# A decoder layer on one core: the first norm's result turned in 32 by 32 blocks on VectorE and through DRAM, and the contraction in quarters

## The chip, the core and the metric

One core of one Trainium2 chip runs the whole kernel. The metric is the device time of one execution in microseconds (us). The engines are TensorE (PE), VectorE (DVE), ScalarE (ACT), GpSimd (POOL) and SyncE (SP), which issues most of the DMAs. Each takes the instructions of its own queue in order.

## The reference

A post-norm decoder layer in float32 over 16 sequences of 512 tokens with 256 features (16 heads of 16; 1024 hidden units). Cut to what matters:

```python
q = query @ wq + query @ Aq @ Bq * 4.0
k = query @ wk
v = query @ wv + query @ Av @ Bv * 4.0
scores = rope(q) @ rope(k).T / sqrt(16)            # per head, causal
a = softmax(scores) @ v @ wo
x1 = layernorm(query + a)                          # the first norm
h = butterfly(x1 @ W_exp + b_exp, up_weights)      # 10 stages over 1024
h = gelu(h + up_bias)
h = butterfly(h, down_weights)
y = h @ W_con + b_con + down_bias
out = layernorm(x1 + y)                            # the second norm
```

## The kernel before

The linear butterflies are folded into the two dense matrices once, at the start (`fold_tasks`), so that each sequence, called a batch, needs x1 times a 256x1024 matrix (`wup`), a gelu, and a 1024x256 matrix (`wdn`).

**Slots.** The order of everything is written out by hand. The loop at the end of `decoder_layer` runs over slots s. A batch begins every 20 slots (`per`), and slot s holds, in this order: the score matmuls of two quads of heads, `largest` (for the row maxima, into the PSUM pair tile `pa` or `pb`) and, 15 slots behind, `weights` (for the exponentials); then `weigh`, which multiplies exponentials into `po`; then the list `others[s]`, filled by `add`; then the list `holes[s]`. Batch b starts at s = 20 b, its attention is finished at s+40, and its feed-forward part runs at s+40 to s+68, beside the attention of the next two batches. The engines keep this order: no scheduler moves anything.

**Scores.** `pa` and `pb` are one buffer each (pools `ps_a`, `ps_b`, bufs=1). Of a `largest` block the VectorE custom reduction L426 reads the scores and leaves a maximum in `mx` (the tile named `junk` is its discarded output); ACT's exponential L488 reads the `weights` blocks, and POOL's select L492 masks them. Slots go round in fives: two with one 512-wide block, two with 384 and 128, one with two of 256, which use both banks for both kinds.

**First norm.** `project_out` (PE) makes attention times `wo` for a tile of 128 tokens, `add_attention` adds it to the tile `z` and takes the statistics (VectorE), `spread` adds epsilon on VectorE and takes the power -0.5 on POOL, `offset` makes -mean/deviation on VectorE, and `centre` applies both on ACT, 4 tiles. The result is x1 with tokens on the partitions. `wup` needs it with features on the partitions: that is `turn_x1`. It makes 4 transposes of 128x128 on PE for each of two halves of the features, one VectorE copy each into `x1T`, and then a POOL add of the output bias to `z`.

**Feed-forward.** `hidden` makes one of 8 chunks of 128 hidden units on PE (8 matmuls of 512 columns), copied to `h` by VectorE (chunks 0 and 4) or ACT; `gelus` runs over all chunks at s+50; `contract` makes a tile of 128 tokens in two halves of 4 chunks, 16 matmuls of 256 columns each, in `py`, and after the second half VectorE adds `py` to `z` and takes the statistics of the second norm. `project_v` makes a tile of the values for a later batch (PE, with a copy by ACT).

**SyncE's queue.** Around s+41 to s+46 it carries, for the next batch, `rows` and `qz<-rows` (row maxima by way of DRAM, L446 and L452), then `sums<-x` and `x<-x` (L546, L550, after ACT has copied `po`), `few<-sums` (L558), and, after a VectorE reciprocal (L564), `recips`, `wide` and `spread` (L566 to L574). PSUM's pool `ps_w` for all other products has 3 buffers.

Of the kernel before, what the change touches and what calls it, by code (L numbers as in the profile page):

```python
# [11 lines left out]
F32 = mybir.dt.float32  # L12
BF16 = mybir.dt.bfloat16
AF = mybir.ActivationFunctionType
ALU = mybir.AluOpType
PSUM = bass.MemoryType.PSUM

P = 128
NH = 16
DH = 16  # L20
HG = 32
NG = P // HG
# [11 lines left out]
def decoder_layer(  # L34
# [18 lines left out]
    nc = tc.nc  # L53
    B, T, D = x.shape
    NT = T // P
    NC = D // P
    DHID = wcon.shape[0]
    NHC = DHID // P
# [5 lines left out]
    ring2 = ctx.enter_context(tc.tile_pool(name="ring2", bufs=2))  # L64
# [3 lines left out]
    dram = ctx.enter_context(tc.tile_pool(name="dram", bufs=4, space=bass.MemoryType.DRAM))  # L68
# [5 lines left out]
    def bank(name, shape):  # L74
        return ps_w.tile(shape, F32, tag="w", name=name)

    def columns(out, w, moving, start, stop):

        for g in range(NG):
            part = slice(HG * g, HG * (g + 1))  # L80
            nc.tensor.matmul(out[part, :], w[:, part], moving, start=start, stop=stop)  # L81
# [10 lines left out]
    xTs, zs = {}, {}  # L92
# [23 lines left out]
    wdn = const.tile([P, NHC, D], F32, name="wdn")  # L116
    bias2 = const.tile([P, 2, D], F32, name="bias2")
# [337 lines left out]
    state = {}  # L455
# [151 lines left out]
    def stats_of(which, b, t):  # L607
        if t == 0:
            state["stats", which, b] = small.tile(
                [P, NT, 2], F32, tag=f"stats{which}", name=f"stats{which}_{b}"  # L610
            )
        bn = small.tile([P, nc.vector.BN_STATS_DIM], F32, tag="bn", name=f"bn{which}_{b}_{t}")
        nc.vector.bn_stats(bn, zs[b][:, t, :])
        nc.vector.bn_aggr(state["stats", which, b][:, t, :], bn)
# [13 lines left out]
    def offset(which, b, t0=0, t1=NT):  # L628
        stats, norm = state["stats", which, b], state["norm", which, b]
        ts = slice(t0, t1)  # L630
        nc.vector.scalar_tensor_tensor(  # L631
            norm[:, 2, ts], stats[:, ts, 0], -1.0, norm[:, 1, ts], ALU.mult, ALU.mult
        )
# [10 lines left out]
            )  # L644


    def turn_x1(b, c):
        if c == 0:
            state["x1T", b] = ring2.tile([P, NC, T], F32, tag="x1T", name=f"x1T_{b}", bufs=1)
        pt = bank(f"pt1_{b}_{c}", [P, NT, P])  # L650
        for t in range(NT):
            nc.tensor.transpose(pt[:, t, :], zs[b][:, t, c * P : (c + 1) * P], ident)  # L652
        nc.vector.tensor_copy(
            state["x1T", b][:, c, :], pt.rearrange("p t q -> p (t q)")
        )
        if c == NC - 1:
            nc.gpsimd.tensor_tensor(
                zs[b],
                zs[b],
                bias2[:, 0:1, :].to_broadcast([P, NT, D]),  # L660
                ALU.add,
            )

    def hidden(b, hc, fused=False):
        if hc == 0:
            state["h", b] = hpool.tile([P, NHC, T], F32, tag="h", name=f"h_{b}")
        ph = bank(f"ph_{b}_{hc}", [P, T])
        for c in range(NC):
            columns(
                ph,  # L670
                wup[:, c, hc * P : (hc + 1) * P],
                state["x1T", b][:, c, :],
                c == 0,
                c == NC - 1,
            )
        h = state["h", b][:, hc, :]
        if fused:
            nc.scalar.activation(h, ph, AF.Gelu, bias=hbias[:, hc : hc + 1])  # L678
        elif hc % 4 == 0:
            nc.vector.tensor_copy(h, ph)  # L680
        else:
            nc.scalar.copy(h, ph)  # L682
# [5 lines left out]
                h[:, hc, :], h[:, hc, :], AF.Gelu, bias=hbias[:, hc : hc + 1]  # L688
            )

    def contract(b, t, half):
        if half == 0:
            state["py"] = bank(f"py_{b}_{t}", [P, D])
        py = state["py"]
        for hc in range(half * NHC // 2, (half + 1) * NHC // 2):
            columns(
                py,
                state["h", b][:, hc, t * P : (t + 1) * P],
                wdn[:, hc, :],
                hc == 0,  # L700
                hc == NHC - 1,
            )
        if half == 1:
            nc.vector.tensor_add(zs[b][:, t, :], py, zs[b][:, t, :])  # L704
            stats_of(2, b, t)

    def store(b):
        nc.sync.dma_start(out[b].rearrange("(t p) d -> p t d", p=P), zs[b])
# [14 lines left out]
    end = B * per + behind  # L723
    last = end + 8
    head = 2
    others = {s: [] for s in range(-head, last)}
    holes = {}
    chains = [(c, side) for c in range(NC) for side in range(2)]

    def add(s, f, *args):  # L730
        others[s].append(lambda: f(*args))

    def start_projection(b, side, c):
        state["pr", b, side, c] = project(b, side, c)
# [13 lines left out]
    for b in range(B):  # L748
        s = b * per
        if b > 0:  # L750

            at = {1: (-16, -11, -13, -9), B - 1: (-3, 2, 10, 10)}.get(b, (-3, -1, 2, 12))
            for t in range(NT):
                add(s + at[t], project_v, b, t)
        if b + 1 < B:

            add(s - head * (b == 0), load_xT, b + 1)
            at = {0: (2, 5, 7, 10), 1: (3, 6, 8, 11)}.get(b, (10, 10, 10, 10))
            for i, (c, side) in enumerate(chains):
                holes.setdefault(s + at[i], []).append(  # L760
                    lambda b=b, side=side, c=c: start_projection(b + 1, side, c)
                )
                turning = s + max(at[0] + 1 + 3 * i, at[i] + 1)
                for step in range(3):
                    add(turning + step, turn, b + 1, side, c, step)
                for step in range(1 + side):
                    add(turning + (6 if i == 3 else 4) + step, part, b + 1, side, c, step)
        add(s + 9, load_x, b)
        add(s + 11, place_largest, b, 0)
        add(s + 21, place_largest, b, 1)  # L770
        for c in range(NC if b + 1 < B else 1):
            if c + 1 < NC:
                add(s + 25 + (b + 1 == B), gather, b, c)
            add(s + (26, 36)[c] + (b + 1 == B), invert, b, c)
            for t in range(NT):
                add(s + ((29, 29, 30, 30), (39, 39, 40, 40))[c][t], scale, b, c, t)
        if b + 1 < B:
            for t in range(NT):
                add(s + (40, 40, 41, 41)[t], project_out, b, t)
                add(s + (40, 40, 41, 42)[t], add_attention, b, t)  # L780
            add(s + 42, spread, 1, b)
            others[s + 43].insert(0, lambda b=b: offset(1, b))
            add(s + 44, centre, 1, b)
            for c in range(NC):
                add(s + 45 + (b + 2 == B), turn_x1, b, c)
        if b + 2 < B:

            late = 2 * (b + 3 == B)
            for hc in range(NHC - late):
                add(s + 46 + hc // 2, hidden, b, hc)  # L790
            holes.setdefault(s + 50, []).insert(0, lambda b=b, late=late: gelus(b, NHC - late))
            for hc in range(NHC - late, NHC):
                holes[s + 50].append(lambda b=b, hc=hc: hidden(b, hc, True))
            for t in range(NT):
                for half in range(2):
                    at = (11, 13, 14, 15, 16, 18, 23, 24)[2 * t + half]
                    if b + 3 == B and t == NT - 1:
                        at = (23, 25)[half]
                    add(s + 40 + at, contract, b, t, half)
            add(s + 65, spread, 2, b)  # L800
            add(s + 67, offset, 2, b)
            add(s + 68, centre, 2, b)
            add(s + 68, store, b)
# [3 lines left out]
    y, z = B - 2, B - 1  # L807
# [4 lines left out]
    for hc, at in ((3, 10), (4, 10), (5, 10), (6, 11), (7, 11)):  # L812
        add(edge + at, hidden, y, hc, True)

    add(end - 3, contract, y, 0, 0)
    add(end - 1, contract, y, 0, 1)
    add(end + 2, contract, y, 1, 0)
    add(end + 2, contract, y, 1, 1)
    for t in range(NT):
        add(end + 2, normalize, z, NC - 1, t)  # L820
    add(end + 2, contract, y, 2, 0)
    for t in range(NT + 1):
        if t < NT:
            add(end + 3, project_out, z, t)
# [2 lines left out]
        if t > 0:  # L827
            add(end + 3, offset, 1, z, t - 1, t)
            add(end + 3, centre, 1, z, t - 1, t)
    add(end + 3, contract, y, 2, 1)  # L830
    add(end + 3, contract, y, 3, 0)
    for c in range(NC):
        add(end + 5, turn_x1, z, c)
    add(end + 5, contract, y, 3, 1)
    for hc in range(NHC):
        add(end + 5, hidden, z, hc, True)
    add(end + 5, spread, 2, y)
# [2 lines left out]
    add(end + 6, store, y)  # L840
    for t in range(NT):
        for half in range(2):
            add(end + 7, contract, z, t, half)
        add(end + 7, finish_tile, z, t)


    first, second = fold_tasks()
# [180 lines left out]
```

## Time and profile before

| | |
|---|---|
| runs | median 1318.08 us of 3 (1312.0 to 1320.54) |
| profiled execution | 1318.97 us, span 1317.0 us, mean granted clock 0.989 |
| busy: PE, DVE, ACT, POOL | 1280.6, 780.5, 702.9, 565.1 us |
| a steady batch | 76.60 us, PE busy 76.37 us |
| transposes L652 | 128, 273 ns each by the median; eight take PE from 552.64 to 553.66 us in batch 5 |
| copies L653 | 32, 678 ns each by the median |

Times in the lines below are us from the start of the span: start, duration, engine, line, operation, output and inputs, shapes, and a count where neighbours are merged; in brackets the idle time before and what ended it. "PEld" is the weight load, "SPq" a DMA issue on SyncE's queue. Matmuls overlap in the array, so starts tell more than durations.

### The profile page before, as it was taken

The page shows a single profiled execution, that of the slowest core. Times are in us where ns is not written, and L with a number is a line of the kernel's source. Part 1 is how long each engine was busy: PE and PEld are TensorE (multiplying, and loading weights), DVE is VectorE, ACT ScalarE, POOL GpSimd, SP SyncE. Part 2 cuts the span into 40 slices and gives each one's busy share as a digit, 9 for nine tenths or more (in the row PEclk, how much of TensorE's full clock was granted, in tenths as well). Part 3 has the DMA queues.
Part 4 walks back from the last instruction along what each step waited for, and adds up shares of the span by engine and source line. Part 5 has one row for each costly group of instructions (what it writes and reads, how often), then busy time and mean ns, then how long its engine had stood idle before and what let it go on. Part 6 is the DMA issues. An engine that isn't in the chain of part 4 may idle for free.

```text
span 1317.0 us, 38318 instructions
## 1 busy us (share of the span) xinstructions
PE 1280.6 (97%) x15896; PEld 575.2 (44%) x15896; DVE 780.5 (59%) x2760; ACT 702.9 (53%) x1047; POOL 565.1 (43%) x905
## 2 busy tenths in 40 slices
PE   8888999999999999999999999999999999999998
PEld 3343435444353544435354443535444353444443
DVE  5776746657465665747566574756657474665431
ACT  2574455555646555564655546465555646455643
POOL 4525325445362544536254453625445362532430
PEclk9889999999999999999999999999999999999999
DMA  5411111111212111121211112121211212111101
GB/s 169 132 32 59 40 49 46 56 56 41 82 41 65 47 56 56 41 83 41 69 42 57 56 41 83 41 67 45 56 56 40 83 41 70 41 40 32 43 20 34
DMA packets 64062, 74.07 MB, mean 56 GB/s; under 512 B 23120, under 2 KB 42576, under 8 KB 63888
## 3 DMA queue, kind: packets, MB, share of 16 engines
q1 hardware_dynamic: 60000, 66.07, 16.0%
q10 hardware_dynamic: 3888, 5.55, 1.4%
q8 instruction: 125, 2.05, 0.7%
q14 instruction: 49, 0.40, 0.1%
HBM read 40.17 MB, written 18.06 MB: 44 GB/s over the span
## 4 chain that ended last, share of the span: by engine, by line
PE 92%; DVE 3%; ACT 2%; DMA 1%; issue 1%; POOL 0%; SPq 0%; POOLq 0%; DVEq 0%; ACTq 0%
PE pb L474 21%; PE py L81 17%; PE ph L81 16%; PE po L516 12%; PE pqk L81 8%; PE pa L417 4%; PE pwo L81 4%; PE pvv L81 4%; DVE junk L426 1%; PE pd L81 1%; PE pt L652 1%; PE pa L474 1%; PE pb L417 1%; ACT pT L488 1%; ACT h L687 0%
## 5 line engine op out<-in xcount | busy, mean ns | idle before, releaser
L426 DVE CUSTOM_DVE_ANT_0 junk<-pa,causal 128x384 bf16<-128x384 f32 (+2 forms) x878 | 438.6, 500 | 339.0 <-PE pa L417 271.6
L488 ACT ACTIVATE pT<-pb 128x1024 f32<-128x1024 f32 (+1 forms) x314 | 294.2, 937 | 354.8 <-PE pa L417 183.8
L492 POOL TENSOR_SCALAR_AFFINE_SELECT pT<-pT 128x256 f32<-128x256 f32 x512 | 202.3, 407 | 651.4 <-ACT pT L488 650.4
L474 PE MATMUL pb<-qz,kz 17*128 17x512 f32 (+2 forms) x1756 | 330.9, 475 | 17.6 <-ACT pT L488 11.7
L417 PE MATMUL pa<-kz,qz 32*128 32x384 f32 (+3 forms) x1756 | 330.6, 476 | 3.4 <-DVE mx L426 3.4
L81 PE MATMUL py<-wdn,h 128*32 128x256 f32 x4096 | 244.3, 381 | 0.0
L81 PE MATMUL ph<-x1T,yb 128*32 128x512 f32 x2048 | 231.6, 594 | 0.2 <-ACT h L678 0.2
L474 PEld LDWEIGHTS pb<-qz,kz 17*128 17x128 f32 (+1 forms) x1756 | 142.4, 184 | 196.4 <-issue 92.3
L516 PE MATMUL po<-pT,vaug 128*32 128x512 f32 (+3 forms) x2048 | 180.9, 447 | 1.8 <-POOL pT L492 1.8
L81 PEld LDWEIGHTS py<-wdn,h 128*32 128x32 f32 x4096 | 125.3, 110 | 99.2 <-issue 12.7
L417 PEld LDWEIGHTS pa<-kz,qz 32*128 32x128 f32 (+1 forms) x1756 | 143.2, 185 | 14.6 <-DVE mx L426 11.6
L81 PEld LDWEIGHTS ph<-x1T,yb 128*32 128x32 f32 x2048 | 63.2, 110 | 139.8 <-issue 107.6
L81 PE MATMUL pqk<-xT,wqk 128*32 128x512 f32 x1024 | 117.6, 608 | 0.0
L682 ACT COPY h<-ph 128x512 f32<-128x512 f32 x84 | 49.2, 585 | 117.3 <-PE ph L81 117.2
L516 PEld LDWEIGHTS po<-pT,vaug 128*32 128x32 f32 x2048 | 47.9, 109 | 105.3 <-issue 59.1
L426 DVE DVE_READ_ACCUMULATOR2_ANT mx<- 128x1 f32 x1024 | 84.6, 83 | 0.0
L638 ACT ACTIVATE z<-z,norm 128x256 f32<-128x256 f32 x128 | 66.7, 589 | 23.2 <-DVE norm L631 23.2
L365 POOL TENSOR_TENSOR swap<-swap,rope_sb 128x512 f32<-128x512 f32 x62 | 78.8, 1270 | 0.0
L426 DVE CUSTOM_DVE_ANT_0 junk<-pb,causal 128x256 bf16<-128x256 f32 (+3 forms) x146 | 63.6, 436 | 16.4 <-PE pb L417 2.5
L687 ACT ACTIVATE h<-h,hbias 128x512 f32<-128x512 f32 x113 | 70.8, 709 | 0.2
L704 DVE TENSOR_TENSOR z<-py,z 128x256 f32<-128x256 f32 x64 | 27.2, 425 | 72.9 <-PE py L81 70.6
L81 PE MATMUL pvv<-wv_sb,xT 128*32 128x256 f32 x1024 | 66.5, 379 | 0.0
(91 smaller groups left out, 1192.1 us busy)
## 6 DMA issues: line engine op xcount, KB each, us to landing
xT<-in_xT SPq DMA_DIRECT2D x16, 512.0 KB
swap<-qz SPq DMA_DIRECT2D x64, 128.0 KB
swap<-kz SPq DMA_DIRECT2D x64, 128.0 KB
z<-in_x SPq DMA_DIRECT2D x16, 512.0 KB
wide<-recips SPq DMA_DIRECT2D x31, 256.0 KB
spread<-wide SPq DMA_DIRECT2D x31, 256.0 KB
out_y<-z SPq DMA_DIRECT2D x15, 512.0 KB
x<-x SPq DMA_DIRECT2D x32, 128.0 KB
```

Of the source, the lines that this page charges most:

```text
L81: nc.tensor.matmul(out[part, :], w[:, part], moving, start=start, stop=stop)
L365: engine.tensor_tensor(swap, swap, rope_sb[:, 1, :], ALU.mult)
L417: lambda i=i, rows=rows, at=at, n=n, t=t, ps=ps: nc.tensor.matmul(ps[:, i, at : at + n], q[rows, par, t * P : n], k_[rows, par, 0:n], star ...
L426: lambda i=i, at=at, n=n, t=t, g=g, ps=ps: nc.vector.tensor_tensor_reduce(out=junk[:, 0:n], in0=ps[:, i, at : at + n], in1=causal[:, T - n ...
L474: lambda i=i, rows=rows, at=at, n=n, k=block, ps=ps: nc.tensor.matmul(ps[:, i, at : at + n], kt[rows, par, k * P : (k + 1) * P], qt[rows, ...
L488: nc.scalar.activation(pT[:, heads, 0:n], ps[:, :, at : at + n], AF.Exp)
L492: nc.gpsimd.affine_select(out=diag, in_=diag, pattern=[[0, 2], [1, P]], compare_op=ALU.is_ge, fill=0.0, base=0, channel_multiplier=-1,)
L516: nc.tensor.matmul(po[HG * g : HG * (g + 1), k * P : T], vaugs[b % 2][:, k, NG * c + g, first : first + HG], pT[:, g, at : at + n], start= ...
L638: nc.scalar.activation(zs[b][:, t, :], zs[b][:, t, :], AF.Identity, bias=norm[:, 2, t : t + 1], scale=norm[:, 1, t : t + 1],)
L682: nc.scalar.copy(h, ph)
L687: nc.scalar.activation(h[:, hc, :], h[:, hc, :], AF.Gelu, bias=hbias[:, hc : hc + 1])
L704: nc.vector.tensor_add(zs[b][:, t, :], py, zs[b][:, t, :])
```

## The change

`turn_x1` is replaced for all batches but the last by `turn_blocks` and `fetch_turned`. `turn_blocks` turns all of `z` on VectorE in one instruction, which transposes each 32 by 32 block in place of the grid; partition j of a group of 32 then holds the features j, 32+j, 64+j and so on for the group's 128 tokens, and four DMAs write them to a DRAM tile in pieces of 512 bytes, one DMA a group. `fetch_turned` reads the DRAM tile back into `x1T` in pieces of 2 KB, with features on the partitions. The tokens lie in another order in `x1T` and so in `h`; `contract` picks its columns by an access pattern.

The steps of the first norm stand in slots 40 and 41 (`add_attention`, two tiles each), 41 (`spread`), 42 (`offset`), 43 (`centre`) and 44 (`turn_blocks`), counted from s; the fetch stands among the holes of slot 45. Before, the last `add_attention` and `spread` stood in 42, `offset` at the head of 43, `centre` in 44 and `turn_x1` in 45 (46 for batch 14). The hidden chunks go from slots 46 to 49 (two each) to the holes of 47, 48 and 49 (2, 3, 3; for batch 13, which has six here, 2, 2, 2). The contraction goes in 16 quarters in place of 8 halves, and three `project_v` of a later batch move. In the built program SyncE's queue has, after `qz<-rows`: four writes `x1rows<-turned`, `sums<-x`, `x<-x`, `few<-sums`, then the fetch `x1T<-x1rows`, then `recips`. VectorE's queue has in slot 44: four reductions L426, the add of `py` of the batch before with its statistics, the turn; then slot 45's reductions. In slot 41 it has the reductions, two adds with statistics, `spread`'s add and the turn of the maxima (`mT`).

```diff
+    def turn_blocks(b):
+
+        state["x1T", b] = ring2.tile([P, NC, T], F32, tag="x1T", name=f"x1T_{b}", bufs=1)
+        turned = ring2.tile([P, D // HG, NT, HG], F32, tag="turned", name=f"turned_{b}", bufs=1)
+        nc.vector.transpose(turned, zs[b].rearrange("p t (k j) -> p k t j", j=HG))
+        rows = dram.tile([D, NG, P], F32, tag="x1rows", name=f"x1rows_{b}")
+        state["x1rows", b] = rows
+        for g in range(NG):
+            nc.sync.dma_start(
+                rows.rearrange("(k j) g q -> j k g q", j=HG)[:, :, g, :],
+                turned[HG * g : HG * (g + 1)].rearrange("j k t i -> j k (t i)"),
+            )
+        nc.gpsimd.tensor_tensor(
+            zs[b],
+            zs[b],
+            bias2[:, 0:1, :].to_broadcast([P, NT, D]),
+            ALU.add,
+        )
+
+    def fetch_turned(b):
+        rows = state.pop(("x1rows", b))
+        nc.sync.dma_start(state["x1T", b], rows.rearrange("(c p) g q -> p c (g q)", p=P))
...
-    def contract(b, t, half):
-        if half == 0:
+    def contract(b, t, first, past):
+        if first == 0:
...
+        h = state["h", b]
+        if b + 1 == B:
+            of = h.rearrange("p c (t g i) -> p c t g i", g=NG, i=HG)
+        else:
+            of = h.rearrange("p c (g t i) -> p c t g i", g=NG, i=HG)
+        for hc in range(first, past):
+            for g in range(NG):
+                nc.tensor.matmul(
+                    py[HG * g : HG * (g + 1), :],
+                    of[:, hc, t, g, :],
+                    wdn[:, hc, :],
+                    start=(hc == 0),
+                    stop=(hc == NHC - 1),
+                )
+        if past == NHC:
...
-            at = {1: (-16, -11, -13, -9), B - 1: (-3, 2, 10, 10)}.get(b, (-3, -1, 2, 12))
+            at = {1: (-16, -11, -13, -9), B - 1: (-3, 2, 10, 10)}.get(b, (-1, 5, 6, 6))
...
-                add(s + (40, 40, 41, 42)[t], add_attention, b, t)
-            add(s + 42, spread, 1, b)
-            others[s + 43].insert(0, lambda b=b: offset(1, b))
-            add(s + 44, centre, 1, b)
-            for c in range(NC):
-                add(s + 45 + (b + 2 == B), turn_x1, b, c)
+                add(s + (40, 40, 41, 41)[t], add_attention, b, t)
+            add(s + 41, spread, 1, b)
+            add(s + 42, offset, 1, b)
+            add(s + 43, centre, 1, b)
+            add(s + 44, turn_blocks, b)
+            holes.setdefault(s + 45, []).append(lambda b=b: fetch_turned(b))
...
-                add(s + 46 + hc // 2, hidden, b, hc)
+                at = s + ((47, 47, 48, 48, 49, 49) if late else (47, 47, 48, 48, 48, 49, 49, 49))[hc]
+                holes.setdefault(at, []).append(lambda b=b, hc=hc: hidden(b, hc))
...
-            for t in range(NT):
-                for half in range(2):
-                    at = (11, 13, 14, 15, 16, 18, 23, 24)[2 * t + half]
-                    if b + 3 == B and t == NT - 1:
-                        at = (23, 25)[half]
-                    add(s + 40 + at, contract, b, t, half)
+            for n, at in enumerate((11, 11, 12, 13, 13, 14, 15, 16, 16, 17, 18, 18, 22, 23, 23, 24)):
+                add(s + 40 + at, contract, b, n // 4, n % 4 * 2, n % 4 * 2 + 2)
```

The last two batches keep the halves, by a helper `halves` that calls `contract` for four chunks.

More of the change, by code (lines that the diff above doesn't have):

```diff
@@ L689, in gelus, with halves @@
             )
-    def contract(b, t, half):
-        if half == 0:
+    def contract(b, t, first, past):
+        if first == 0:
             state["py"] = bank(f"py_{b}_{t}", [P, D])
         py = state["py"]
[L695 to L703, printed above, removed]
+        h = state["h", b]
[13 more added lines that the diff above has]
+        if past == NHC:
             nc.vector.tensor_add(zs[b][:, t, :], py, zs[b][:, t, :])
             stats_of(2, b, t)
+    def halves(b, t, half):
+        contract(b, t, half * NHC // 2, (half + 1) * NHC // 2)
     def store(b):
@@ L813, in decoder_layer @@
         add(edge + at, hidden, y, hc, True)
[L815 to L818, printed above, removed]
+    add(end - 3, halves, y, 0, 0)
+    add(end - 1, halves, y, 0, 1)
+    add(end + 2, halves, y, 1, 0)
+    add(end + 2, halves, y, 1, 1)
     for t in range(NT):
         add(end + 2, normalize, z, NC - 1, t)
-    add(end + 2, contract, y, 2, 0)
+    add(end + 2, halves, y, 2, 0)
     for t in range(NT + 1):
@@ L829, in decoder_layer @@
             add(end + 3, centre, 1, z, t - 1, t)
-    add(end + 3, contract, y, 2, 1)
-    add(end + 3, contract, y, 3, 0)
+    add(end + 3, halves, y, 2, 1)
+    add(end + 3, halves, y, 3, 0)
     for c in range(NC):
         add(end + 5, turn_x1, z, c)
-    add(end + 5, contract, y, 3, 1)
+    add(end + 5, halves, y, 3, 1)
     for hc in range(NHC):
@@ L842, in decoder_layer @@
         for half in range(2):
-            add(end + 7, contract, z, t, half)
+            add(end + 7, halves, z, t, half)
         add(end + 7, finish_tile, z, t)
```

## The prediction

> **What bounds the kernel now.** I read the busy shares on the page first, then the stretches by batch, then the instructions in order of time around one turn, then the DMA queue's issues there.
>
> ```profile
> PE 1280.6 (97%) x15896; PEld 575.2 (44%) x15896; DVE 780.5 (59%) x2760; ACT 702.9 (53%) x1047; POOL 565.1 (43%) x905
> ```
>
> ```profile
> 478.25:554.85 76.60, 76.37 (x973) 34.56 (x976) 46.90 (x169) 42.21 (x61) 35.11 (x57) 1.00 0.18 56
> ```
>
> The second fence is one steady batch: 76.60 us, then busy us of TensorE 76.37, weight loads, VectorE 46.90, ScalarE, GpSimd, then the clock, 1.00. So TensorE (PE) sets the time, taking its instructions in order; whatever makes it wait is lost, and whatever leaves it is gained. Below I follow batch 5, whose slots s+41 to s+47 I call 41 to 47. Slots 42 to 46 begin on PE at 541.01, 543.95, 547.07, 551.00 and 553.66.
>
> ```profile
> 541.69 0.18 DVE L444 STREAM_TRANSPOSE mT<-mx 128x32 f32<-128x32 f32 x1
> 542.25 0.56 DVE L426 CUSTOM_DVE_ANT_0 junk<-pa,causal 128x384 bf16<-128x384 f32 x1 [0.38 <-PE pa L417]
> 544.00 0.08 DVE L426 DVE_READ_ACCUMULATOR2_ANT mx<- 128x1 f32 x1
> 544.00 0.42 DVE L603 TENSOR_TENSOR z<-pwo,z 128x256 f32<-128x256 f32 x1
> ...
> 544.14 0.59 PE L417 MATMUL pa<-kz,qz 16*128 16x384 f32 x2
> ...
> 550.25 0.08 DVE L426 DVE_READ_ACCUMULATOR2_ANT mx<- 128x1 f32 x1
> 551.14 0.42 DVE L704 TENSOR_TENSOR z<-py,z 128x256 f32<-128x256 f32 x1 [0.80 <-PE py L81]
> 552.64 1.09 PE L652 MATMUL pt<-ident,z 128*128 128x128 f32 x8
> 553.66 0.70 PE L474 MATMUL pb<-qz,kz 17*128 17x512 f32 x2
> ```
>
> Two things matter here. The first score matmul into pa in slot 43 starts at 544.14, just after VectorE (DVE) has read the last of the old pa (544.08): pa is one buffer, and DVE is already only just in time. And the eight transposes hold PE from 552.64 to 553.66, 1.02 us.
>
> ```profile
> 537.93 0.43 SPq L96 DMA_DIRECT2D xT<-in_xT  x1
> ...
> 553.76 0.54 SPq L546 DMA_DIRECT2D sums<-x  x1
> 554.40 0.54 SPq L550 DMA_DIRECT2D x<-x  x1
> 555.52 0.32 SPq L558 DMA_DIRECT2D few<-sums  x1
> ```
>
> These are SyncE's issues: a load of the shape of the fetch (512 KB into 128 partitions in 2 KB pieces), and the three that the new order places between the four writes and the fetch.
>
> **The change, term by term (batch 5's clock).**
>
> A, removed: the transposes, 15 of 16 batches: **-1.02** each. The two copies L653 (1.27 us on DVE) go too; they cost PE nothing now, since the next junk reduction, ready at 554.85, began at 554.90.
>
> B, the fourth add_attention moved from 42 to 41 and spread with it. In the built order DVE then runs, after tile 2's statistics (541.69): tile 3's add, bn_stats and aggregate (1.02, as 540.67 to 541.69), spread's add (0.2), mT (0.18), and only then slot 42's four reductions, which start at 543.1 in place of 542.25 and take their 1.83 as before: done at 544.94. PE, which has slot 42's quarter (half of a 1.87 half, so 0.95) where project_v (0.97) stood, is ready at 543.9 and can't write pa until 545.0 in place of 544.14: **+0.86**. If another engine covered it this would be 0; none does, for PE is in order.
>
> On the other queues the steps cost nothing. POOL's pow now waits for DVE until 543.0 with the swap multiply (1.27), two selects and the kz add behind it; the select that slot 44 needs is ready near 548.0 and PE asks for it at 549.1. ACT's centre (2.06) in slot 43 ends near 549.1, before slot 44's exponentials can start (549.4). Without either cover it would cost up to 1 us a batch.
>
> C, quarters: the same 4,096 matmuls at the same size. But slots 44 and 54 (blocks of 256, which DVE reads out of both banks) held a half each and get a quarter. Such a slot with a 0.97 filler is visible at 531.23 to 534.60: 3.37 long for 3.07 of work. So **+0.28** in each, +0.56. In slot 44, from 547.93: PE is through at 550.97, DVE at 551.2, and slot 45 starts at 551.25.
>
> D, the turn on DVE. The trace has no 128x1024 turn. Bounds: 0.18 (mT, 32 columns) and 32 of those, 5.8; nearest are the reductions (512 columns 0.69, 128 columns 0.29, so 1.04 ns a column), which gives 1.2, close to the two copies it replaces. Its place is what counts: behind slot 44's reductions and behind the last py add with its statistics (1.10, waiting for PE), so 552.35 to 553.55, ahead of slot 45's reductions, which PE would have been ready for at 552.4. They end at 555.0; PE, done with slot 45 (scores 1.07, po 0.57, project_v 0.97) at 553.86, gets pa at 555.06: **+1.20**. With 0.2 for the turn it is 0.2; with 2.4, what POOL's 128x1024 add takes, 2.4. The 5.8 would be 4.6 more a batch, +64 in all; I leave it to the 2 in 10 outside the range, because the 32 columns' 0.18 is hardly more than the 0.17 of a 128x4 instruction and so nearly all start-up.
>
> E, the way through DRAM. Four writes: an issue takes 0.32 to 0.55 in the rows above; I take 0.43 with the gap, because out_y's store, whole rows of a tile, has 0.38. Writes 553.6 to 555.3. Then sums (555.3), x (0.64 later), few, which waits for sums as now (1.76 after it): 557.1. The fetch goes at 557.45; the writes have landed (x's 128 KB took 2.0). xT's load kept the DMA engines busy until 541.4, 3.5 after its issue, and a landing follows: 3.6 to 4.2. So x1T is there at 561.0 to 561.7; I take 561.3. PE from 555.06: scores 1.05, two project_v 1.95, slot 47's scores and po 1.96, ready at 560.0: **+1.3**. With issues and landing at their short ends 0.5, at their long ends 2.4. The reciprocal behind few on DVE lands at about 558.8 and ends before slot 47's reductions can start (559.2): nothing, or 0.6 if few is 1 us later. The bias add (2.38 on POOL) now waits for the turn, with slot 45's select and the second norm's pow behind it; they end by 557.9 and PE needs the select at 559.1. Behind the fetch in SyncE's queue stand recips, wide and spread, later by some 1.5; spread landed by 566 and the scale that reads it runs in slot 49, after 568.5. The hidden chunks, two a slot in 46 to 49, become 2, 3 and 3 in 47 to 49, and the project_v that leave 42 and 52 fill 45 and 46: the same work on PE, and h's copies (0.58 on ACT, two or three a slot beside at most 3.1 us of other ACT work in slots over 6 us long) keep up.
>
> Sum: -1.02 + 0.86 + 0.56 + 1.20 + 1.30 = **+2.9 a batch**, for batches 1 to 13: +37.7. Batch 0 has fold work in slots 41 to 45 that covers half: +1.5. Batch 14 has its last fetch among weights alone. There the hidden start at 1240.37 with few issued at 1239.97, and the fetch goes behind few: near 1240.4 + 3.8 = 1244.2, against 1239.35 without transposes, so +3.9. In all +43.1 on the profiled execution's 1318.97 (span 1317.0): **1362.1 us**. The median of the runs, 1318.08, is 0.9 below that execution; I leave it so.
>
> [...]
>
> **The rivals.** (1) The waits are all covered: DVE's added work fits into its 30 us of idle a batch and the fetch lands in time, so that only A stays. 15 x 1.02: **1303.7**. For it: DVE 59% busy, the three slots between turn and hidden. Against: 544.08 to 544.14, where DVE is already last. It decides if pa is released by 554 in slot 46 and x1T there by 558. (2) The turn and the fetch are short (D 0.2, E 0), and B and C eat up A: +0.4 x 15, **1325**, no difference. For it: every price in D and E is a bound from other shapes. (3) The DMA way is long: small pieces and four issues in a row put the fetch 2 us later, E 3.3: 1362 + 14 x 2 = **1390**. For it: wide, 256 KB, took 4 us from issue to the next issue (559.18 to 563.15). Against: xT.
>
> **How the numbers follow.** Forecast 0.63, rival 1 0.09, rival 2 0.13, rival 3 0.15. About 1% (13 us) is what the runs, 1312.0 to 1320.54, can tell from nothing. Faster by over 1% is rival 1: 0.09. Rival 2 and the edge of the forecast: 0.13 within 1%. Slower 0.78. D from 0.2 to 2.4 is -14 to +17 us and E from 0.5 to 2.4 is -11 to +15; two short ends together reach 1337. To leave out only 2 in 10 I go from 1328 to 1388.
>
> **What would show it.** After: a steady batch of 79.5 us with PE busy less than before by 1.0; slot 43's first pa matmul 0.9 late, released by mx; a turn of 1.2 us just after the py add; slot 46's pa released by mx again; the first ph of each batch waiting about 1.3 us for a DMA into x1T. Wrong it would be if ph starts without a wait, if the transposes' microsecond is simply gone from the 76.6, or if the turn stands ahead of slot 44's end on DVE.

## The result and the profile after

The changed kernel takes 1388.18 us in the median of four runs (1380.16 to 1394.04), the kernel before 1316.22 beside it (1312.0 to 1320.54): the ratio is 1.054, with an interval from 1.047 to 1.062. It is slower by 72 us. The profiled execution took 1383.64 us (span 1381.9), 64.7 more than the profiled one before. The forecast was 1362.1 with a range up to 1388, so the direction is right, the size is a third short, and the median lies on the range's upper edge, 0.2 us past it.

The page of after: busy time by engine, the shares of the chain that ended last, and two of the costliest groups (busy us and mean ns, then the idle time before them and what ended most of it).

```profile
PE 1305.4 (94%) x15776; PEld 570.2 (41%) x15776; DVE 786.9 (57%) x2745; ACT 703.0 (51%) x1047; POOL 564.1 (41%) x905
...
PE 78%; DMA 8%; DVE 6%; ACT 2%; issue 2%; SPq 2%; POOL 1%; DVEq 0%; POOLq 0%; ACTq 0%
...
L81 PE MATMUL ph<-x1T,yb 128*32 128x512 f32 x2048 | 240.7, 618 | 32.5 <-DMA x1T<-x1rows 32.3
...
L417 PEld LDWEIGHTS pa<-kz,qz 32*128 32x128 f32 (+1 forms) x1756 | 143.6, 184 | 35.7 <-DVE mx L426 29.2
```

120 matmuls are gone, and yet PE, which was busy for 97% of the span, is busy for 94%. The hidden chunks (`ph`) wait 32.3 us for the fetch, where before the same matmuls had 0.2 us of idle time before them in all; the scores' wait for `mx` has gone from 11.6 to 29.2. DMA has gone from 1% to 8% of the chain.

Two batches of after in the view of stretches (length, then busy us of PE, weight loads, DVE, ACT and POOL, the granted clock, DMA share, GB/s), and the first 4 us of the hidden chunks that open each of them:

```profile
494.73:575.96 81.23, 77.66 (x960) 34.14 (x961) 47.34 (x167) 42.21 (x60) 35.03 (x55) 1.00 0.22 65
820.24:902.62 82.38, 79.92 (x960) 34.31 (x960) 48.14 (x174) 42.22 (x60) 34.99 (x55) 0.98 0.21 65
575.96:579.96 4.00, 4.00 (x37) 1.24 (x41) 0.69 (x1) 0.29 (x1) 0.00 (x0) 1.00 0.25 66
820.24:824.24 4.00, 4.00 (x24) 1.04 (x28) 1.33 (x8) 0.00 (x0) 0.00 (x0) 0.62 0.19 70
```

A batch is 81.2 or 82.4 us long in place of 76.60. The last two lines show a difference that the forecast does not have at all: after the wait in batch 8 the granted clock is 0.62 over 4 us (0.50 from 819.90 to 823.31), and 24 matmuls start where batch 5 has 37. Over batches 1 to 13 the eight periods without such a fall average 80.78 us (80.22 to 81.26), the five with one 82.58.

Batch 5 of after in order of time, where the forecast had its steps (slots 43, 44, 46, 47):

```profile
558.15 0.19 PEld L417 LDWEIGHTS pa<-kz,qz 16*128 16x128 f32 x2 [0.60 <-DVE mx L426]
...
564.29 0.42 DVE L733 TENSOR_TENSOR z<-py,z 128x256 f32<-128x256 f32 x1
...
565.39 1.25 DVE L651 STREAM_TRANSPOSE turned<-z 128x1024 f32<-128x1024 f32 x1
...
568.01 0.30 PEld L417 LDWEIGHTS pa<-kz,qz 32*128 32x128 f32 x4 [0.65 <-DVE mx L426]
...
575.96 3.64 PE L81 MATMUL ph<-x1T,yb 128*32 128x512 f32 x32 [2.88 <-DMA x1T<-x1rows]
```

Everything stands where it was put: slot 43's `pa` waits for `mx`, the turn lasts 1.25 us and follows the last `py` add, slot 46's `pa` waits for `mx`, and the first `ph` waits for the fetch, but 2.9 us and not 1.3.

One sign of the forecast did not come: PE is busy for 77.66 us of this batch, 1.3 more than before and not 1.0 less. In the kernel with the early fetch below, whose batch is 1.5 us longer than before's, PE's idle time is 0.7 us and its busy time 77.43: the profile counts most of the short waits for `pa` and `pb` as busy, so the transposes' microsecond can't be read off the busy time.

The DMA issues of the same stretch, and the chain of waits from them to `ph`:

```profile
566.66 1.85 SPq L655 DMA_DIRECT2D x1rows<-turned  x4
568.62 0.54 SPq L546 DMA_DIRECT2D sums<-x  x1
569.20 0.55 SPq L550 DMA_DIRECT2D x<-x  x1
570.87 0.34 SPq L558 DMA_DIRECT2D few<-sums  x1
572.26 0.39 SPq L668 DMA_DIRECT2D x1T<-x1rows  x1
```

```profile
568.04 4.07 DMA x1rows<-turned
...
572.26 3.66 DMA x1T<-x1rows
...
575.96 3.64 PE ph L81 x32
```

The turn ends at 566.64. The four issues take 1.85 us for a forecast 1.7. The fetch goes 5.62 us after the turn's end in place of 3.9, here because the fourth write landed only 4.07 us after its issue. In 11 of the 13 batches the fetch goes at 4.46 to 4.80, held by `few` in front of it. Over the 13, `ph` starts 8.2 to 9.35 after the turn's end (mean 8.69) in place of 7.75.

### The profile page after: what moved, and what is told of

Read it like the earlier page. It is cut to its first block, busy times and chain, and to the rows that moved or that the text cites. A ratio compares the mean times of both kernels' runs of the same rounds, so it can differ in the third digit from the quotient of the medians.

```text
span 1381.9 us, 38196 instructions
## 1 busy us (share of the span) xinstructions
PE 1305.4 (94%) x15776; PEld 570.2 (41%) x15776; DVE 786.9 (57%) x2745; ACT 703.0 (51%) x1047; POOL 564.1 (41%) x905
## 3 DMA queue, kind: packets, MB, share of 16 engines
q1 hardware_dynamic: 80400, 81.80, 19.6%
## 4 chain that ended last, share of the span: by engine, by line
PE 78%; DMA 8%; DVE 6%; ACT 2%; issue 2%; SPq 2%; POOL 1%; DVEq 0%; POOLq 0%; ACTq 0%
PE ph L81 16%; PE pb L474 16%; PE py L725 16%; PE po L516 9%; PE pqk L81 8%; PE pa L417 5%; DMA x1T<-x1rows 4%; PE pwo L81 4%; DVE junk L426 3%; DMA sums<-x 2%; SPq L655 1%; PE pvv L81 1%; PE pa L474 1%; ACT pT L488 1%; DVE turned L651 1%
## 5 line engine op out<-in xcount | busy, mean ns | idle before, releaser
L426 DVE CUSTOM_DVE_ANT_0 junk<-pa,causal 128x384 bf16<-128x384 f32 (+2 forms) x878 | 436.6, 497 | 310.8 <-PE pa L417 255.4
L81 PE MATMUL ph<-x1T,yb 128*32 128x512 f32 x2048 | 240.7, 618 | 32.5 <-DMA x1T<-x1rows 32.3
L725 PE MATMUL py<-wdn,h 128*32 128x256 f32 x4096 | 251.8, 381 | 0.0
L417 PEld LDWEIGHTS pa<-kz,qz 32*128 32x128 f32 (+1 forms) x1756 | 143.6, 184 | 35.7 <-DVE mx L426 29.2
L426 DVE DVE_READ_ACCUMULATOR2_ANT mx<- 128x1 f32 x1024 | 84.7, 83 | 0.0
L426 DVE CUSTOM_DVE_ANT_0 junk<-pb,causal 128x256 bf16<-128x256 f32 (+3 forms) x146 | 63.6, 436 | 15.7 <-PE pb L417 2.5
L703 DVE COPY h<-ph 128x512 f32<-128x512 f32 x29 | 20.1, 692 | 83.6 <-PE ph L81 83.6
```

The costliest lines, as they stand in the source:

```text
L417: lambda i=i, rows=rows, at=at, n=n, t=t, ps=ps: nc.tensor.matmul(ps[:, i, at : at + n], q[rows, par, t * P : n], k_[rows, par, 0:n], star ...
L426: lambda i=i, at=at, n=n, t=t, g=g, ps=ps: nc.vector.tensor_tensor_reduce(out=junk[:, 0:n], in0=ps[:, i, at : at + n], in1=causal[:, T - n ...
L725: nc.tensor.matmul(py[HG * g : HG * (g + 1), :], of[:, hc, t, g, :], wdn[:, hc, :], start=(hc == 0), stop=(hc == NHC - 1),)
```

## The experiments

All have the kernel before beside them in the same series (medians 1312.80 to 1317.69). In the theories A to E are the terms of the prediction: A the transposes gone, B the norm's slots, C the quarters, D the turn on DVE, E the way through DRAM.

### One part alone: the quarters

The kernel before, with `contract` in quarters, their slots and those of `project_v` from the change.

```diff
-at = {...}.get(b, (-3, -1, 2, 12))            # project_v
+at = {...}.get(b, (-1, 5, 6, 6))
-at = (11, 13, 14, 15, 16, 18, 23, 24)[2 * t + half]
-add(s + 40 + at, contract, b, t, half)
+for n, at in enumerate((11, 11, 12, 13, 13, 14, 15, 16, 16, 17, 18, 18, 22, 23, 23, 24)):
+    add(s + 40 + at, contract, b, n // 4, n % 4 * 2, n % 4 * 2 + 2)
```

> The kernel before with one part of the change alone: the contraction in quarters in its new slots and project_v in its new slots. The PE transposes, the norm's slots and the hidden chunks stay as before. My prediction prices this at +0.28 in slots 44 and 54 (C), so +0.56 x 13 = +7: 1323 to 1326 with a steady batch of 77.2. Rival a: the quarters cost nothing because the next slot's PE work makes it up, 1316 to 1319, steady batch 76.6. Rival b: the spread of fillers is the larger part of the loss and opens more waits than the two slots that I counted, 1335 or more, steady batch 78 or more.

Measured: 1332.13 us (ratio 1.0106, 1.0067 to 1.0145), a steady batch of 77.67: C is **1.07** a batch and not 0.56. The instructions of this kernel around three slot starts say where:

```profile
554.42 0.08 DVE L426 DVE_READ_ACCUMULATOR2_ANT mx<- 128x1 f32 x1
554.61 0.70 PE L474 MATMUL pb<-qz,kz 17*128 17x512 f32 x2 [0.23 <-ACT z L638]
...
600.18 0.60 ACT L488 ACTIVATE pT<-pa 128x512 f32<-128x512 f32 x1 [0.22 <-DVE mx L426]
601.11 0.08 DVE L426 DVE_READ_ACCUMULATOR2_ANT mx<- 128x1 f32 x1
601.26 0.29 PEld L474 LDWEIGHTS pb<-qz,kz 17*128 17x128 f32 x3 [0.68 <-ACT pT L488]
...
603.91 0.30 PEld L474 LDWEIGHTS pb<-qz,kz 17*128 17x128 f32 x4 [0.41 <-ACT pT L488]
603.94 0.08 DVE L426 DVE_READ_ACCUMULATOR2_ANT mx<- 128x1 f32 x1
604.08 0.30 PEld L417 LDWEIGHTS pa<-kz,qz 32*128 32x128 f32 x4
```

These are the starts of slots 45, 55 and 56. I had counted the two slots whose blocks DVE reads out of both banks (44 and 54). Both are 3.37 us long, as forecast, where before they had 3.93 and 3.94: each gives back 0.56 for a quarter that is 0.94 of work, so 0.38 is lost in each in place of 0.28. The next slot's `pb` starts 0.1 us after DVE's last read (554.50 and 601.19); before, it started 0.67 after it at slot 55. The brackets name ScalarE, but its exponential had ended at 600.78, half a microsecond before the load, and its `centre` ran on past 554.61.

But slot 55 lost a quarter too, from 3.37 to 2.62, and slot 56 grew by 0.15: 0.34 lost in a place that I didn't count. It is DVE again. Its reads of slot 55's `pa` end at 604.02, and slot 56's `pa` starts at 604.08, 0.17 behind its `pb`; before, `pa` started beside `pb`, 0.71 after DVE's last read. 0.38 + 0.38 + 0.34 = 1.10. The first rival falls; the second has the reason, another wait than the two counted, but not the size.

### One part alone: the steps of the norm

```diff
-add(s + (40, 40, 41, 42)[t], add_attention, b, t)
-add(s + 42, spread, 1, b); others[s + 43].insert(0, offset ...); add(s + 44, centre, 1, b)
+add(s + (40, 40, 41, 41)[t], add_attention, b, t)
+add(s + 41, spread, 1, b); add(s + 42, offset, 1, b); add(s + 43, centre, 1, b)
```

> The kernel before with one part of the change alone: the fourth add_attention and spread in slot 41, offset in 42, centre in 43. Transposes on PE, halves and project_v as before. My prediction prices this (B) at +0.86 x 13 = +11: 1327 to 1331, steady batch 77.5, slot 43's first pa matmul late and released by mx. Rival a: 0, because with halves and project_v in slot 42 PE itself is late enough: 1316 to 1319. Rival b: the wait for pa passes on to ScalarE's exponentials and costs twice that, 1338 or more.

Measured: 1327.58 us (ratio 1.0075, 1.0051 to 1.0099), a steady batch of 77.30: B is **0.70**. Slot 43 is 3.82 us long in place of 3.12 and every other slot as before. Its first `pa`:

```profile
542.25 0.19 PEld L417 LDWEIGHTS pa<-kz,qz 16*128 16x128 f32 x2 [0.60 <-DVE mx L426]
```

The mechanism is the one forecast, place and releaser included; the rivals fall.

### Without the wait for the way through DRAM

```diff
 def turn_blocks(b):
     ...
     state["x1rows", b] = rows
+    if b > 0:
+        fetch_turned(b)          # takes state["x1rows", b - 1]
     for g in range(NG):
         nc.sync.dma_start(rows..., turned...)
```

> The kernel after, but the fetch into x1T takes the rows that the batch before wrote (so the output differs from the reference's) and is issued ahead of the four writes: nothing waits for this batch's way through DRAM, while the turn, the writes, the other transfers and every instruction of the engines stay. It removes E and, with it, the stretches at half clock that follow the wait before ph in batches 3, 7, 8, 10, 12, 13 and 14. Theory: E with its clock falls is 2.1 + about 1 us a batch, and A, B, C and D are as I priced them (-1.02, +0.86, +0.56, +0.93 to 1.20), so what is left is +1.3 to +1.6 a batch: 1334 to 1342, steady batch 78.0, no wait before ph, clock 1.00. Rival: the loss is mostly in B, C and D or spread over other waits and the way through DRAM is only where it shows, 1360 or more.

This kernel (called e3 in the texts below) takes the other batch's rows into `x1T`: it leaves out the wait for this batch's transfers, not the transfers.

Measured: 1343.70 us (ratio 1.0193, 1.0165 to 1.0221), 44.5 below after and just above the theory's range; the steady batch is 78.08, `ph` waits for nothing, and from the first hidden chunks (175.73 us) to 1188 us the clock stays at 1.00. A steady batch:

```profile
488.11:566.23 78.12, 77.43 (x965) 34.32 (x961) 47.31 (x168) 42.21 (x61) 35.00 (x55) 1.00 0.23 68
```

So A, B, C and D together are 78.08 - 76.60 = **+1.48** a batch, and the way through DRAM is the rest, nearly two thirds of the loss. The rival is out.

### The same without the turn

```diff
-turned = ring2.tile([P, D // HG, NT, HG], F32, tag="turned", name=f"turned_{b}", bufs=1)
-nc.vector.transpose(turned, zs[b].rearrange("p t (k j) -> p k t j", j=HG))
...
-    turned[HG * g : HG * (g + 1)].rearrange("j k t i -> j k (t i)"),
+    zs[b][HG * g : HG * (g + 1)].rearrange("j t (h q) -> j (t h) q", h=2),
```

> The kernel with the early fetch of old rows (e3), and without the turn on VectorE: the writes take the untransposed z, in pieces of the same size (another part of the computation left out). What it gains on 1343.7 is D alone. My prediction prices the turn at +1.20 a batch in slot 46's wait for pa; from the traces of after and of the early fetch I now expect 0.75 a batch: 1331 to 1335, steady batch 77.35, slot 46's pa no longer released by mx. Rival: the reductions would be late in slot 45 without the turn too, behind the last py add: under 0.2 a batch, 1341 to 1345.

Measured: 1332.86 us, 10.8 below the kernel with the early fetch. The batch of the same number:

```profile
564.24:641.60 77.36, 76.67 (x964) 34.13 (x960) 45.39 (x167) 42.06 (x61) 35.01 (x55) 1.00 0.25 69
```

D is 78.08 - 77.36 = **0.72**; slot 46 shrinks from 3.80 to 3.08 us and slot 45 keeps its length (2.62). The sum closes: -1.02 + 0.70 + 1.07 + 0.72 = +1.47, against +1.48 measured with all four in place.

### PE work in the gap

```diff
+def fill(b):
+    pf = bank(f"pf_{b}", [P, 3 * P])
+    for n in range(2):
+        columns(pf, wup[:, 0, n * P : (n + 1) * P], wup[:, 1, 0 : 3 * P], True, True)
...
+if hc == 0:
+    holes.setdefault(at, []).append(lambda b=b: fill(b))
 holes.setdefault(at, []).append(lambda b=b, hc=hc: hidden(b, hc))
```

> The kernel after with some 1.4 us of matmuls (eight 32x384 by two passes, into a bank that nobody reads) ahead of each batch's first hidden chunk, in the time in which PE waits for x1T (1.7 to 2.9 us). Theory: the half clock after that wait comes from PE's idle time, so that the shorter gap (0.3 to 1.5 us) no longer brings it: no stretch at 0.5, mean clock 0.99, and some 13 to 16 us less than after, 1370 to 1377, with runs that agree better. Rival: the clock falls for another reason, or PE's lead is not what sets ph's start: 1386 to 1392 with the falls still there. Third: the fill is longer than the gap where x1T is early, up to +0.3 a batch, which would show as a batch without a wait for the DMA.

Measured: 1380.67 us (1378.49 to 1382.25), 7.5 below after's median and with a spread of 4 us in place of 14. From the first hidden chunks (172.91 us) to 1219 us there is no stretch at half clock left (mean clock of its runs 0.986 to 0.987, of after's 0.972 to 0.982). Batch 8, whose first hidden chunks ran at 0.62 in after, by order of time and by its first 4 us:

```profile
818.23 1.47 PE L81 MATMUL pf<-yb 128*32 128x384 f32 x16
821.54 1.02 PE L81 MATMUL ph<-x1T,yb 128*32 128x512 f32 x5 [1.84 <-DMA x1T<-x1rows]
```

```profile
821.54:825.54 4.00, 4.00 (x37) 1.41 (x40) 0.69 (x1) 0.30 (x1) 0.00 (x0) 1.00 0.20 66
```

PE still stands for 1.84 us, and the clock stays at 1.00; in after PE stood for 2.61 us there, so the fall goes with the length of PE's idle time (more on it at the end). The gain is half of what I expected (13 to 16). Five falls at 1.7 us are 8.5, which is what the profiled after had to lose; the rest of my figure was falls in batches 13 and 14, which this kernel still has. And x1T comes later here, `ph` 8.97 us after the turn's end in place of 8.69, so that batches 1 to 13 are only 5 us shorter in all than those of after.

### The fetch first in the queue

```diff
     for g in range(NG):
         nc.sync.dma_start(rows..., turned...)
+    fetch_turned(b)
...
-holes.setdefault(s + 45, []).append(lambda b=b: fetch_turned(b))
```

> The kernel after with the fetch issued directly behind the four writes, ahead of sums, x and few: SyncE then stands until the writes have landed. It tells whether the fetch of after was late for its place in the queue or for the writes. By the prediction's prices (a landing of 2.0 us) the fetch goes 3.4 us after the turn's end in place of 4.6, x1T comes 1.2 us earlier, the wait before ph falls from 2.1 to 0.9 us with no half clock behind it: 1355 to 1364. Rival: the writes need 3 to 4 us from the last issue, so that the fetch still goes 4.5 to 5.5 us after the turn's end: 1380 to 1392, and sums, x and few come some 3 us later without a further cost.

Measured: 1382.97 us (1377.11 to 1388.27), within what after's own runs span. The time is the rival's, but the fetch goes 3.94 to 4.07 us after the turn's end in ten of 13 batches and at 4.6 to 5.45 in three: between the two. Batch 4:

```profile
486.04 1.85 SPq L655 DMA_DIRECT2D x1rows<-turned  x4
490.07 0.38 SPq L669 DMA_DIRECT2D x1T<-x1rows  x1
490.84 0.55 SPq L546 DMA_DIRECT2D sums<-x  x1
```

SyncE stands from 487.89 to 490.07 for the fourth write, which was issued at 487.43: it landed within 2.6 us. So the writes allow a fetch at +4.0 and `few` in after one at +4.5 to 4.8; the queue's order costs 0.6 of the 0.9 us by which x1T is late. Five batches show it with periods of 79.72 to 79.90, against 80.78; in most of the others x1T came later (`ph` up to 9.12 after the turn's end, for 7.4 to 7.8 in these five), and two have stretches at half clock.

### Another shape of the same trip

```diff
-rows = dram.tile([D, NG, P], ...)              # four writes, 32 partitions x 8 x 512 B
+rows = dram.tile([P, NG, NC * P], ...)         # one write, 128 partitions x 4 KB
+nc.sync.dma_start(rows, turned.rearrange("p k c t i -> p k (c t i)"))
...
-nc.sync.dma_start(state["x1T", b], rows.rearrange("(c p) g q -> p c (g q)", p=P))
+for k in range(NG):                            # four fetches, 32 partitions x 4 x 1 KB
+    nc.sync.dma_start(
+        state["x1T", b][HG * k : HG * (k + 1)].rearrange("j g c q -> j g (c q)"),
+        rows[:, k, :].rearrange("(g j) q -> j g q", j=HG))
```

> The kernel after with another shape of the way through DRAM, the same bytes: one write of 128 partitions x 4 KB in place of four of 32 partitions x 8 x 512 B, and four fetches of 32 partitions x 4 x 1 KB in place of one; the turn is two instructions of 128x512 for that. Same places in the schedule. Theory (E is made of issues, landings and the queue, not of a fixed latency of DRAM): the write is out 0.4 us after the turn's end in place of 1.9 and few comes 1.5 us earlier, the last fetch goes near +4.9 and lands 2 to 2.5 later, x1T at +7.4 in place of +8.3 to 9.4: wait before ph under 1 us, no half clock, 1352 to 1366. Rival: the DMA engines or DRAM set the trip, and x1T comes as late as before: 1380 to 1392.

Measured: 1368.56 us (1367.45 to 1370.95), 19.6 below after; the theory's sign, and just above its range. Batch 4's issues (turn's end 486.56):

```profile
486.58 0.32 SPq L658 DMA_DIRECT2D x1rows<-turned  x1
487.18 0.53 SPq L546 DMA_DIRECT2D sums<-x  x1
...
489.74 1.81 SPq L669 DMA_DIRECT2D x1T<-x1rows  x4
```

`ph` starts 7.7 to 8.6 us after the turn's end (mean 8.07), 0.6 sooner than in after, the periods of batches 1 to 13 average 80.08, and up to 1210 us no wait is followed by half clock (mean clock of its runs 0.984 to 0.988). The same bytes in another shape are worth 20 us in the medians; of the 18 us by which batches 1 to 13 of the two profiled executions differ, about half is the clock.

### Can the rest be covered?

The next three (the first is called e8 in the texts, the second e9) keep the turn and the way through DRAM (in the last shape), put B and C back, and move PE work of slot 50 into the gap: projections of the next batch in slots 45, 46 and 47, ahead of the hidden chunks.

```diff
-at = {0: ..., 1: ...}.get(b, (10, 10, 10, 10))     # start_projection
+at = {0: ..., 1: ...}.get(b, (5, 6, 7, 10))
-late = 2 * (b + 3 == B)                            # hidden chunks in slot 50, Gelu fused
+late = 2
```

> A version that keeps the turn and the way through DRAM (one write, four fetches) and undoes the rest: halves and project_v in the slots of before (C), the fourth add_attention and spread back in 42 with offset first in 43 and centre behind it in 43 (B), and in place of project_v three of the four projections of the next batch, 2.05 us each, out of slot 50 into 45, 46 and 47 ahead of the hidden chunks (D and E covered by PE work); two hidden chunks with their Gelu go to slot 50 in place of them. Theory: the losses were waits, and with PE work in their place only A is left or a part of it: 1303 to 1316. Rival: ScalarE's Gelus, now beside less PE work in slot 50, or an x1T that is still late give 1 us or more a batch back: 1318 to 1340.

Measured: 1342.06 us (ratio 1.0179, 1.0138 to 1.0221), a steady batch of 77.8: the rival, and 2 us more than its range. Slot 51 takes 4.59 us in place of 2.94:

```profile
589.63 1.45 PEld L729 LDWEIGHTS py<-wdn,h 128*32 128x32 f32 x32 [1.36 <-ACT h L705]
...
592.54 0.19 PEld L474 LDWEIGHTS pb<-qz,kz 32*128 32x128 f32 x2 [1.46 <-ACT pT L488]
```

With three projections gone from slot 50, ScalarE's Gelus lie open. The next kernel has `late = 3` and two `project_v` of the last batch in other slots.

> e8 with two edits: a third hidden chunk with its Gelu in slot 50, and for the last batch two project_v in slots 46 and 47 of batch 13 in place of slot 50. In e8's steady batch (77.8) slot 51 takes 4.59 us in place of 2.94, because ScalarE's eight Gelus and two table loads (1.28 each) last until 591.46 while TensorE is through with slot 50 at 587.95. Theory: a chunk more (1.9 us of PE work) in slot 50 covers that, -1.65 x 13 = -21, and batch 13 gains up to 3: 1316 to 1322, steady batch 76.2. Rival: the third fused chunk only makes the Gelus or the banks (three for work) the bound, so that slot 50 grows by what slot 51 gives back: 1338 to 1345, steady batch 77.8.

Measured: 1329.73 us (ratio 1.0135, 1.0104 to 1.0167), a steady batch of 77.32. Both halves happened: slot 51 is back at 2.94, and slot 50 grew to 9.7, because the projection now waits for a bank:

```profile
501.06 1.92 PE L81 MATMUL pqk<-xT,wqk 128*32 128x512 f32 x16 [0.99 <-ACT h L705]
```

The last version puts that projection ahead of the chunks, and `centre` into slot 44 behind its exponentials.

> e9 with two orders changed: in slot 50 the projection stands ahead of the three hidden chunks (in e9's slot 50 it waits 0.99 us for a bank that ScalarE's Gelus free late), and centre stands in slot 44 behind its exponentials (in e9 it holds them up until 468.9 and slot 44 takes 4.23 us in place of 3.93). Theory: both are waits, -1.0 and -0.3 a batch, steady batch 76.0 against 76.6 of before, so that what is left of the change is a part of A: 1308 to 1313 with before at 1313 to 1318, ratio 0.993 to 0.998. Rival: the bank is short in either order (py's first half in slot 51 then waits for it) and the turn comes later with centre, so that x1T is late again: steady batch 77.0 or more, 1322 to 1332.

Measured: 1328.75 us (ratio 1.0083, 1.0054 to 1.0111), the rival's time, with a steady batch between the two, 76.5 to 77.5. One of the two shortest:

```profile
950.99:1027.49 76.50, 76.06 (x961) 34.53 (x965) 47.12 (x168) 40.44 (x57) 35.05 (x55) 1.00 0.23 69
```

So 1.02 us of PE work less buys 0.1 on before's 76.60: slots 46, 47 and 51 are 0.45, 0.2 and 0.27 longer than their work. In 46 `pa` starts 0.46 behind `pb`, after DVE's reads; 51 ends with a wait for ScalarE's exponential, which stands behind the Gelus there. `py` itself, which the rival named, starts on time. The first batch also reaches its hidden chunks at 180.45 in place of e9's 171.39, which I did not follow up. No version of mine beats the kernel before.

## Why the prediction was right, and where it was wrong

**A, B and D: right in mechanism, B and D too large.** A was not run alone, but the sum closes with it. B was +0.86 and is 0.70. D was +1.20 and is 0.72, though the turn was 1.25 us for a forecast 1.2: its place in DVE's queue was right, but the wait that it makes is shorter than the instruction. Without the turn DVE stands idle for 0.35 us before slot 45's reductions (557.52 to 557.87 in that kernel), and with it they start 0.75 later, not 1.25; I had read a spare 0.05 (552.35 against 552.4).

**C: mis-sized, 0.56 for 1.07.** The mechanism is the one forecast, DVE's reads of the scores. The step that failed is the count: I looked only at the two slots whose blocks lie in both banks, and slots 55 and 56, with their 512-wide blocks, are held by DVE too once a quarter is gone from slot 55. By chance B, C and D err against each other: A to D were +1.60 a batch, and are +1.48.

**E: mis-sized, 1.30 for 2.70.** This is the term that made the forecast short, and it lies above the 2.4 that I gave for its long end. What failed is the arrival of x1T, and most of that in SyncE's queue. In the mean of batches 1 to 13 `few` goes 4.18 us after the turn's end in place of 3.55 (the writes take 1.95 to issue in place of 1.7, and `few` follows `sums` by 2.09 in place of 1.76), the fetch 0.59 behind `few` in place of 0.35, and `ph` 3.92 behind the fetch in place of 3.85: 8.69 in place of 7.75. The landing of 2.0 us that I took from `x` (128 KB) is too short as well, 2.6 for the fourth write in batch 4 of the kernel with the fetch first and 4.07 in batch 5 of after, but only in batch 5 does the fetch wait for it. 80.78 - 78.08 = 2.70 is the whole price in batches without a fall of the clock. Of it 2.37 is the wait before `ph`, in the mean of these eight. Most of the rest is at its edge: PE's last matmul before the wait ends 6.44 us after the turn's end (573.08 in batch 5; the forecast had 6.45), but with no wait `ph` overlaps it and starts at 6.26.

**The clock: missing.** I costed PE's wait at its own length. In the profiled execution five of the 13 waits were followed by 3.41 us at half clock (0.50), 1.7 us of PE work each: 8.5 of the 21.5 us by which that execution exceeds the forecast. In the runs of 1391 and 1392.3 us of span the mean clock was 0.974 and 0.972 in place of 0.982; (0.982 - 0.972) x 1392 = 14 us of clock more, an estimate of eight more falls, for a span 10 us longer. So after's spread of 14 us goes with the clock, and the two kernels whose waits bring no fall, the filled one and the one write, spread over 4 us. The profiled execution lies 4.5 us below the median.

Together, for batches 1 to 13: forecast 37.7, measured 61.5. The 1.28 too little a steady batch (80.78 for 79.5; E 1.40 too small, A to D 0.12 too large) is 16.6, the five periods with a fall add 1.80 each, 9.0, and before's own longer periods (998 us for 13 x 76.60) take 1.8 off: 61.5. Batch 0 cost nothing in place of +1.5, batch 14 and the end +3.4 in place of +3.9, but not by the way forecast: the fetch of batch 14 goes ahead of `sums` and `few`, at 4.06 us after the turn's end, and there are stretches at half clock there that before does not have.

That the time still lies at the range's edge is partly luck: the range had room for a turn that costs 2.4, which cost 0.72, and E and the clock, neither of them within its bounds, used that room up.

**The rivals.** The third, 1390, has the time almost to the microsecond, but only part of its reason: the fetch went 0.6 to 0.9 us later than forecast and not 2 (1.4 and 1.7 in two of 13), and the clock brought much of the rest. Its claim that small pieces and four issues matter is borne out by the kernel with one write, 0.6 us. The first rival fell: B, C, D and E all cost something. So did the second: E was not 0.

## What to carry to other kernels

A wait on the bounding engine had two prices here, its length and what the clock did after it: 3.41 us at half clock behind five of after's 13 waits, those with 2.04 us and more of idle time in one step of the clock, and runs 14 us apart in place of 4. Cost the second wherever a wait of about 2 us is expected, and expect a spread between runs from it. A small piece of work on a bound engine may be the filler of a slot whose other engines are just as long: before counting it as a gain, ask what bounds that slot next, in every slot that loses work and not only in those where an engine was already seen to be tight. And check the engine that a profile names for a wait against its own end: where it had long been done, another one held the wait. A trip through memory is the sum of its issues (1.95 us here), its place in the queue (the fetch at 4.77 after the turn's end) and two landings (2.6 for a write, `ph` 3.92 behind the fetch), each to be priced under the load of its own stretch.

## What the runs showed of the hardware

**In after, a fall of the clock follows idle time within one step of 3.413 us.** In the profiled after the falls begin at 413.72, 737.98, 819.90, 983.74 and 1147.58 us and last 3.41 each, at a clock of 0.50; the distances are 95, 24, 48 and 48 times 3.413. So the five lie on one grid of 3.413 us, while the batches are 80.22 to 83.12 us long. Between 165 and 1170 us of after, PE's idle time summed within one step of that grid tells the falls from the rest: 2.04, 2.27, 2.40, 2.55 and 2.90 us were followed by half clock over the next step, 1.94, 1.81 and all less were not. Batch 5's wait of 2.88 us fell on two steps, 1.07 and 1.81, and the clock stayed at 1.00. Outside that stretch this does not hold: in the first 165 us and from 1180 us on, around batches 13 and 14, the clock also falls with less idle time (0.66 us before the fall at 140.65 of after, 0.60 before the one at 1297.77); why, these runs do not show.

**A turn of 128x1024 in 32 by 32 blocks took VectorE 1.25 us** (15 of them, 1.242 to 1.247), and two of 128x512 in a row 1.27 (e8, at 558.06). Between the 1.246 of 1024 columns and the 0.18 of the 128x32 turn (before, at 541.69) that is 1.07 ns a column, an estimate, which leaves 0.15 us for the start: of the 0.18 us of the 128x32 turn its columns are then only 0.03, as the forecast had taken it.
